# Split query and key operands for steps 3 and 4 of the first attention unit, and a later place for the second chunk's layer normalisation

## The chip, the cores and the metric

The kernel runs on one core of a Trainium2 chip. The metric is the time on the device in microseconds, median of several runs. TensorE (PE) multiplies matrices into PSUM, VectorE (DVE) and ScalarE (ACT) work on SBUF and PSUM, GpSimd (POOL) on SBUF alone, and SyncE (SP) issues the DMAs. Each engine takes its instructions in the order in which the program issued them, and waits at one whose inputs are not there yet.

## The reference

Layer normalisation, causal attention with 32 heads of 16, and a gate from a linear layer with routed low-rank corrections, on x of 2 x 1024 x 512 in float32:

```python
x = L0_attn_x                       # (2, 1024, 512)
xn = _layernorm(x, axis=-1)
q, k, v = (xn @ W.T + b for each)   # 32 heads of 16
scores = einsum('bhqd,bhkd->bhqk', q, k) / sqrt(16)
att = softmax(where(causal, scores, -inf))
s = (att @ v) @ Wo.T + bo
g = silu(xn @ W_base.T + b_base + top-2-of-8 routed rank-16 update)
return x + s * g
```

## The kernel before, in words

**Tiling.** The two sequences of 1024 tokens are cut into chunks of 512: (b, c). The heads are taken in four groups of 8 (oc). A *unit* (b, oc, c) is the attention of one group's heads for one chunk of queries. The first units are (0,0,0), (0,1,0), (0,0,1), (0,1,1). A unit is cut into *steps*; each step computes scores for some pieces of keys and queries (`scores`, L1714 on), takes their exponential on ScalarE in two instructions of 128 x 1024 (`pt`), masks the diagonal blocks on GpSimd (`masked`, L1756), and one step later multiplies by the values on TensorE (`values`, L1780). A unit of the first chunk has five steps: 0 and 1 take 512 columns for the even and the odd heads, 2 and 3 take pieces of 384 and 128 columns for the even and the odd heads, and 4 takes twice 256. So the plan's steps 0 to 4 are the first unit, and 5 to 9 the second. Score tiles have two PSUM buffers and a step uses both.

**Score operands.** All units but the first use *split* operands: queries and keys are cut into a rounded high part (`fp32r`) and a remainder, and a score is the sum of two reduced-precision matmuls. The heads of a pair share 32 rows, so the high parts and the remainders are interleaved: `split_keys` and `split_queries` write the high part on ScalarE and the remainder on VectorE, `copy_remainder` copies it on ScalarE, and `place_keys` and `place_queries` exchange rows by two DMAs each. The first unit, in `first_task`, uses whole float32 operands for all its five steps: `queries` writes two query tiles on VectorE, one for each parity of the heads with the other's rows zeroed, `keys` writes the keys on ScalarE. Its keys are split later (`apart`), since the third unit, the second chunk's queries for the same heads, reads them as split keys; `apart` shuffles the rows into pairs first, because `first_task` projects with weights in their plain order.

**Order.** The order of all instructions is written out by a planner when the program is built. The main loop issues, for each step n, the scores of n, the values of n-1, the masks of n, and then `fill(n)`: pieces of the other tasks (projections, values, gates, outputs). Inside `fill`, tasks with TensorE work come first, then the functions in the list `later` whose step has come, then those in `urgent`, and last the tasks without TensorE work. `turns` are called at its very start. A task gives way with `yield WAIT` (until the next fill) or `PAUSE`. `room` counts free buffers. The planner's own clock (`Metered`, `Queue`) decides only whether some of these functions are put off by a step; line L56 of the profile is the helper that issues nearly all VectorE and ScalarE instructions, L72 the one that issues SyncE's DMAs, L258 the helper of most matmuls.

**The stage at hand.** `early_values` (fills 0 to 2) makes the first chunk's values by a seven-product scheme on blocks: its products are p1, p2, p6, p7, p4, each followed by an addition on VectorE, and its last additions prepare the sums for p5 and p3 (`early_rest`, fills 3 and 4). In fill 2, behind `early_values`, `qk_task` projects queries and keys of the second unit (0,1,0) and splits them; its query remainder `qT<-qf,qT` on VectorE stands between two ScalarE operations. `layernorm_task(0, 1)` normalises the second chunk of the first sequence: statistics (fill 0), the power for the reciprocal deviation on GpSimd (L282), normalisation and the transposes of the first half in 32 x 32 blocks (fill 1), with a store of them to DRAM and four DMAs that bring them back with the blocks in place; the second half follows in fill 2. First read of the result: the projection of the third unit in fill 6.

Of the kernel before, what the change touches and what calls it, by code (L numbers as in the profile page):

```python
# [8 lines left out]
F32 = mybir.dt.float32  # L9
F32R = mybir.dt.float32r  # L10
# [21 lines left out]
NEG = -3.0e38  # L32
NF = 2 + 4 * 2 * 4
WARM = 10


Z_LOW, Z_HIGH = 1.0e-20, 1.0e20
# [60 lines left out]
def direct(ctx, tc, sound, x, wq, wk, wv, wo, wb, wa, wg, wB, bq, bk, bv, bo, bb, out):  # L98
# [148 lines left out]
    WAIT = object()  # L247
    PAUSE = object()
    turned_at, now = {}, [0]
    xns, xnTs, kTs, qTs, vs, gs, oTs, kfs = {}, {}, {}, {}, {}, {}, {}, []  # L250

    def mm_tile(name):
        return ps_mm.tile([P, D], F32, tag="mm", name=name)
# [42 lines left out]
    def layernorm_task(b, c):  # L296


        xt = chunk_tile(b, c)
        for i in range(NS):  # L300
            i0 = c * C + i * P
            sp.dma_start(
                out=xt[i * SQ : (i + 1) * SQ],
                in_=x[b, i0 : i0 + P].rearrange("(t r) d -> r t d", r=SQ),
            )
        if b == 0:
            load_rest()
        tiles = [xt[:, t] for t in range(TT)]
        for _ in range(3 if b else 1):
            yield WAIT  # L310
        s = yield from statistics(tiles, True)
        if b:
            yield WAIT
        for t in range(0, TT, 2):
            normalize(tiles[t : t + 2], s[0][:, t : t + 2], s[1][:, t : t + 2])
            yield PAUSE
        if b:
            yield WAIT
        xnT = sb.tile([P, KC, C], F32, tag="xnT", bufs=3, name=f"xnT_{b}_{c}")
        for k0 in range(0, KC, 2):  # L320
            sq = sb.tile([P, 2, NS, TT, SQ], F32, tag="sq", bufs=1, name="sq")
            for t in range(TT):
                yield PAUSE
                ve.transpose(
                    out=sq[:, :, :, t],
                    in_=tiles[t][:, k0 * P : (k0 + 2) * P].rearrange(
                        "p (k q d) -> p k q d", k=2, q=NS
                    ),
                )
            scr = dram.tile([NS, SQ, 2, NS, TT * SQ], F32, tag="scr", name="scr")  # L330

            def store(sq=sq, scr=scr, place=None):
                sp.dma_start(
                    out=scr.rearrange("i d k q m -> (i d) (k q m)"),
                    in_=sq.rearrange("p k q t r -> p (k q t r)"),
                )
                if place:
                    behind.append(place)
                    landed(place, now[0] + 3)

            def place(k0=k0, scr=scr):
                for q in range(NS):
# [9 lines left out]
            if not b:  # L352
                store()
                place()
                yield WAIT
                continue
            later.append((now[0] + b, lambda s=store, p=place: s(place=p)))
            for _ in range(0 if k0 else 1 + b):
                yield WAIT
        xnTs[b, c] = xnT  # L360

    def first_task():
# [4 lines left out]
        xnTs[0, 0], qTs[0, 0, 0] = xnT, qT  # L367
        kfs.append(kT)
# [60 lines left out]
        project_first(pq, wqks[0][:, 2 * KC : 3 * KC], TT - 1)  # L429
        queries(0)  # L430
        queries(1)
        ve.stream_shuffle(b_pair, b_sb, PAIRED)
        ve.tensor_tensor(b_less, b_pair[:, 0:KC], b_pair[:, KC:], ALU.subtract)
        project_first(pk, wqks[0][:, 3 * KC :], 3)
        keys(1, TT)
        kTs[0, 0, 0] = sb.tile([P, 2, C], F32R, tag="kT", bufs=4, name="kT_0_0_0")
        low = sb.tile([P, C], F32, tag="rb", bufs=1, name="low_0_0_0")

        def apart():
            ve.stream_shuffle(low, kT, PAIRED)  # L440
            split_keys(kTs[0, 0, 0], low, low)
            later.append((now[0] + 1, lambda: place_keys(kTs[0, 0, 0], low)))

        later.append((0, lambda: pair_up(wqks[1])))
        paired = lambda: pair_up(wqks[0])
        costs[paired], costs[apart] = (1.1, 5), (1.1, 6)
        later.append((3, paired))
        later.append((4, apart))
        yield 8 * MM

    def qk_task(b, oc, c):
# [401 lines left out]
    def early_values():  # L853

        at, raw, t, s = early_at["x"], early_at["w"], early_at["t"], early_at["s"]
        vt = value_tile(0, 0)
        for i in range(TT):
            vs[0, i] = vt[:, i]
        hv = heads(vt)
        early_at["v"] = slot = lambda i, j: hv[:, 2 * i : 2 * i + 2, H // 2 * j : H // 2 * (j + 1), 0:HD]  # L860
        s11, s12, s21, s22 = slot(0, 0), slot(0, 1), slot(1, 0), slot(1, 1)
        ve.tensor_tensor(s[1], at(1, 1), s[2], ALU.subtract)
        p1 = yield from early_product("p1", at(0, 0), raw[0, 0])
        early_add(s12, p1, early_bias(0))
# [12 lines left out]
        early_add(s21, p4, s21)  # L877
        ve.tensor_tensor(s[0], s[1], at(0, 0), ALU.add)
        ve.tensor_tensor(s[3], at(0, 1), s[1], ALU.subtract)
        ve.tensor_tensor(s12, s12, early_bias(1), ALU.add)  # L880

    def early_rest():

# [603 lines left out]
    for b in range(NB):  # L1487
        for c in range(NC):
            s0 = starts[b, 0, c]
            xn = [("xnT", b, c)]  # L1490
            if not b and not c:
                room["x"] -= 1
                Task(1, first_task(), 8 * MM, takes={"xnT": 1, "qT": 1, "kT": 1}, uses=xn)
            else:
                Task(
                    s0 - (12 if c else 25) if b else -9, layernorm_task(b, c), 0.0, after=s0 - (44 if c == 0 else 30) if b else -9,
# [217 lines left out]
    def scores(n):  # L1714
# [1 line left out]
        place_urgent(n)  # L1716
        ss = [ps_s.tile([P, 2, C], F32, tag="s", name=f"s{p}") for p in range(2)]
        for m, (par, kt, q0, w, col) in enumerate(pieces):
            first_unit = (b, oc, c) == units[0]
            halves = 1 if first_unit else 2  # L1720
            keys = kfs[0] if first_unit else kTs[b, oc, kt // TT][:, par]
            q = qTs[b, oc, c]
            for half_ in range(halves):
                for s in range(4):
                    rows = slice(32 * s, 32 * s + 32)
# [581 lines left out]
```

## Time and profile before

| | |
|---|---|
| median of 3 runs | 543.24 us (543.08 to 543.8) |
| profiled execution, its own time | 543.99 us |
| its span, first to last instruction | 542.2 us |
| granted TensorE clock | 0.995 |
| TensorE busy | 532.7 us (98%) |
| VectorE busy | 341.2 us (63%) |
| ScalarE busy | 351.4 us (65%) |
| GpSimd busy | 115.5 us (21%) |
| steps 3 and 4 of the first unit, start of scores | 37.35 and 41.16 us |
| first score of the second unit | 44.96 us |

Times are from the span's start. In a timeline a row gives start, duration, engine, line, operation, what is written and read, and in brackets the idle time of the engine before it and what ended it. Rows of one kind that follow one another are merged, with their count behind an x. Consecutive instructions of an engine overlap by some hundredths of a microsecond, so starts are better compared with starts. In the chain that ended last, durations are counted without overlap.

### The profile page before, as it was taken

Reading aid. Unit: us, or ns where it says so; the run is one execution under the profiler, and the core shown is the slowest. Engines: PE = TensorE matmul, PEld = TensorE weight load, DVE = VectorE, ACT = ScalarE, POOL = GpSimd, SP = SyncE. Lnnn points to the kernel's source line nnn. Section 1 sums busy time; section 2 is a strip of 40 time slices with the busy share of each in tenths; the row PEclk is TensorE's granted clock in tenths of the full one; section 3 lists DMA queues with packets and bytes.
Section 4 is the critical chain, followed back from the end, with each engine's and each line's share of the span. In section 5 each row is a group of like instructions: output and inputs, shape, how many; then the busy total and the mean of one; then the engine's idle time right before and its main releaser. Section 6 shows DMA issues by size and latency. Waiting matters only on the chain.

```text
span 542.2 us, 19903 instructions
## 1 busy us (share of the span) xinstructions
PE 532.7 (98%) x8623; PEld 284.1 (52%) x8623; DVE 341.2 (63%) x706; ACT 351.4 (65%) x387; POOL 115.5 (21%) x249
## 2 busy tenths in 40 slices
PE   8999999999999999999999999999999999999994
PEld 8546445544455554454555554454645564455672
DVE  5763586665584886566369766574276554749843
ACT  2457755777776766757667756657667776877640
POOL 2212401021033322030133320130113330121200
PEclk9999999999999999999999999999999999999997
DMA  8636366366526574813666545640124121753311
GB/s 252 158 110 211 133 165 223 91 197 205 160 99 215 195 226 155 230 42 100 187 169 199 186 135 171 195 149 24 63 97 143 61 85 28 253 169 91 101 41 48
DMA packets 67744, 78.15 MB, mean 144 GB/s; under 512 B 9928, under 2 KB 52944, under 8 KB 67136
## 3 DMA queue, kind: packets, MB, share of 16 engines
q1 hardware_dynamic: 67632, 76.78, 45.5%
q8 instruction: 70, 1.15, 0.9%
q14 instruction: 26, 0.21, 0.1%
q10 hardware_dynamic: 16, 0.00, 0.0%
HBM read 45.34 MB, written 19.37 MB: 119 GB/s over the span
## 4 chain that ended last, share of the span: by engine, by line
PE 97%; DVE 1%; DMA 1%; issue 0%; SPq 0%; POOL 0%; POOLq 0%
PE av L1780 26%; PE p L258 26%; PE s L1728 18%; PE q L258 14%; PE ph L258 3%; PE po L258 2%; PE pk L258 1%; PE pq L258 1%; PE warm L213 1%; PE pq_first L388 1%; PE h L258 1%; PE pk_first L388 1%; DMA kept<-w_gate 1%; PE pt_o L258 0%; PE pt_x L378 0%; DVE g L56 0%
## 5 line engine op out<-in xcount | busy, mean ns | idle before, releaser
L56 ACT ACTIVATE pt<-s 128x1024 f32<-128x1024 f32 x288 | 290.5, 1024 | 149.1 <-PE s L1728 145.6
L1756 POOL TENSOR_SCALAR_AFFINE_SELECT pt<-pt 128x256 f32<-128x256 f32 (+1 forms) x224 | 106.8, 491 | 400.0 <-ACT pt L56 399.5
L1780 PE MATMUL av<-pt,v 128*32 128x512 f32 (+3 forms) x1680 | 154.6, 467 | 0.1
L1728 PE MATMUL s<-qT,kT 32*128 32x512 f32 (+3 forms) x1616 | 106.6, 363 | 0.0
L1728 PEld LDWEIGHTS s<-qT,kT 32*128 32x128 f32 x1616 | 61.1, 183 | 56.6 <-issue 34.6
L1780 PEld LDWEIGHTS av<-pt,v 128*32 128x32 f32 x1680 | 40.8, 109 | 53.8 <-issue 38.5
L258 PE MATMUL p<-wt,asum 128*32 128x256 f32 x960 | 58.4, 379 | 0.0
L258 PE MATMUL q<-asum,wqk 128*32 128x256 f32 x832 | 51.1, 379 | 0.0
L258 PEld LDWEIGHTS p<-wt,asum 128*32 128x32 f32 x960 | 31.1, 110 | 29.2 <-issue 12.6
L258 PE MATMUL q<-xnT,wqk 128*32 128x256 f32 x624 | 39.5, 379 | 0.0
L258 PEld LDWEIGHTS q<-asum,wqk 128*32 128x32 f32 x832 | 26.8, 110 | 23.7 <-issue 6.6
L258 PEld LDWEIGHTS q<-xnT,wqk 128*32 128x32 f32 x624 | 20.2, 110 | 18.4 <-issue 6.6
L56 DVE SCALAR_TENSOR_TENSOR kf<-q,kf 128x256 f32<-128x256 f32 x39 | 16.5, 422 | 20.6 <-PE q L258 20.0
L56 DVE TENSOR_TENSOR g<-p,g 128x512 f32<-128x512 f32 x20 | 13.8, 688 | 22.8 <-PE p L258 22.6
L258 PE MATMUL p<-w,xnT 128*32 128x256 f32 x448 | 27.6, 379 | 0.0
L56 DVE TENSOR_TENSOR v<-p,v 128x512 f32<-128x512 f32 x22 | 15.0, 684 | 14.0 <-PE p L258 13.9
L258 PE MATMUL p<-w,asum 128*32 128x256 f32 x320 | 20.9, 379 | 0.0
L258 PEld LDWEIGHTS p<-w,xnT 128*32 128x32 f32 x448 | 14.9, 110 | 10.6 <-issue 3.3
L258 PEld LDWEIGHTS ph<-wag_sb,xnT 128*32 128x32 f32 x512 | 15.2, 110 | 3.9 <-issue 3.0
L56 DVE TENSOR_TENSOR x<-p,x 128x512 f32<-128x512 f32 x15 | 10.3, 685 | 10.4 <-PE p L258 10.4
L258 PE MATMUL ph<-wag_sb,xnT 128*32 128x136 f32 x512 | 16.6, 279 | 0.0
L56 DVE TENSOR_TENSOR g<-p,bb_sb 128x512 f32<-128x512 f32 x8 | 5.5, 690 | 17.2 <-PE p L258 17.1
(159 smaller groups left out, 577.5 us busy)
## 6 DMA issues: line engine op xcount, KB each, us to landing
wt<-kept SPq DMA_DIRECT2D x36, 256.0 KB
qT<-qT SPq DMA_DIRECT2D x30, 256.0 KB
x<-in_x_dram SPq DMA_DIRECT2D x16, 256.0 KB
kept<-wqk SPq DMA_DIRECT2D x16, 256.0 KB
wqk<-kept SPq DMA_DIRECT2D x4, 1024.0 KB
kT<-kf SPq DMA_DIRECT2D x30, 128.0 KB
scr<-sq SPq DMA_DIRECT2D x6, 512.0 KB
xnT<-scr SPq DMA_DIRECT2D x24, 128.0 KB
```

The source lines that it names most:

```text
L56: return getattr(self.engine, name)(*args, **named)
L213: nc.tensor.matmul(warm[:, n % 4 * P : n % 4 * P + P], lhsT=ident, rhs=ident, start=True, stop=True)
L258: nc.tensor.matmul(o[j : j + 32], lhsT=lhsT[:, j : j + 32] if len(lhsT.shape) == 2 else lhsT[:, j // 32], rhs=rhs, start=start, stop=stop,)
L388: nc.tensor.matmul(ps[:, cols], lhsT=w[:, k, :], rhs=xnT[:, k, cols], start=k == 0, stop=k == KC - 1)
L1728: nc.tensor.matmul(ss[s // 2][:, s % 2, col : col + w], lhsT=keys[rows, kt % TT * P : kt % TT * P + P], rhs=q[rows, halves * par + half_, ...
L1756: nc.gpsimd.affine_select(out=d, in_=d, compare_op=ALU.is_ge, fill=0.0, base=0, pattern=[[0, d.shape[1]], [1, P]], channel_multiplier=-1,)
L1780: nc.tensor.matmul(avs_now[par][32 * s : 32 * s + 32, q0 : q0 + w], lhsT=vs[b, kt][:, h * VS - HD * par : h * VS - HD * par + HP], rhs=pt[ ...
```

## The change

The first unit uses whole operands in steps 0 to 2 only (`SPLIT_FROM = 3`). For steps 3 and 4 its queries and keys are split like those of the other units. For that, ScalarE writes the queries with their bias from PSUM once more (`qf`), and `apart`, now in fill 0 instead of fill 6, shuffles both queries and keys into pairs on VectorE and splits both; the keys' placement, the queries' remainder and the queries' placement follow in fill 1. `first_task` takes both query buffers, and gives one back at the start of fill 2.

The second chunk's layer normalisation is moved for the first sequence. Its statistics are in fill 1 and no longer fill 0, with the power straight behind them. Normalisation and the first half's transposes and store (`begin`, `half(0)`) are called at the end of `early_values`, in fill 2, so that on VectorE they stand ahead of `qk_task`'s remainders. The placement of the first half is issued at the end of fill 2, and the second half's transposes, store and placement in fill 3.

```diff
+SPLIT_FROM = 3
...
     def layernorm_task(b, c):
-        for _ in range(3 if b else 1):
+        for _ in range(3 if b else 2):
             yield WAIT
-        s = yield from statistics(tiles, True)
-        if b:
+        s = yield from statistics(tiles, bool(b))
+        if b == 0:
+            xnT = sb.tile([P, KC, C], F32, tag="xnT", bufs=3, name=f"xnT_{b}_{c}")
+
+            def begin():
+                normalize(tiles, *s)
+                early_at["turn"] = half(0)
+
+            def half(k0):
+                sq = sb.tile([P, 2, NS, TT, SQ], F32, tag="sq", bufs=1, name="sq")
+                for t in range(TT):
+                    ve.transpose(
+                        out=sq[:, :, :, t],
+                        in_=tiles[t][:, k0 * P : (k0 + 2) * P].rearrange(
+                            "p (k q d) -> p k q d", k=2, q=NS
+                        ),
+                    )
+                scr = dram.tile([NS, SQ, 2, NS, TT * SQ], F32, tag="scr", name="scr")
+                sp.dma_start(
+                    out=scr.rearrange("i d k q m -> (i d) (k q m)"),
+                    in_=sq.rearrange("p k q t r -> p (k q t r)"),
+                )
+                return lambda: place_half(k0, scr)
+
+            def place_half(k0, scr):
+                for q in range(NS):
+                    sp.dma_start(
+                        out=xnT[q * SQ : (q + 1) * SQ, k0 : k0 + 2].rearrange(
+                            "d k (i m) -> d k i m", i=NS
+                        ),
+                        in_=scr[:, :, :, q].rearrange("i d k m -> d k i m"),
+                    )
+                if k0:
+                    turned_at[b, c] = now[0] + int((sp.landing() - sp.now) / 3.4)
+
+            early_at["begin"] = begin
+            while "turn" not in early_at:
+                yield WAIT
+            early_at["turn"]()
             yield WAIT
+            half(2)()
+            xnTs[b, c] = xnT
+            return
...
     def first_task():
         queries(0)
         queries(1)
+        qf = sb.tile([P, C], F32, tag="qf", bufs=2, name="qf_0_0_0")
+        act.activation(qf, pq, AF.Identity, bias=bq_sb[:, 0:1])
...
-        kTs[0, 0, 0] = sb.tile([P, 2, C], F32R, tag="kT", bufs=4, name="kT_0_0_0")
+        q2, k2 = split_tiles(0, 0, 0)
         low = sb.tile([P, C], F32, tag="rb", bufs=1, name="low_0_0_0")
+        turns.append((SPLIT_FROM - 1, lambda: room.update(qT=room["qT"] + 1)))
 
         def apart():
+            qs = sb.tile([P, C], F32, tag="qf", bufs=2, name="qs_0_0_0")
             ve.stream_shuffle(low, kT, PAIRED)
-            split_keys(kTs[0, 0, 0], low, low)
-            later.append((now[0] + 1, lambda: place_keys(kTs[0, 0, 0], low)))
+            ve.stream_shuffle(qs, qf, PAIRED)
+            split_keys(k2, low, low)
+            split_queries(q2, qs)
+            later.append((now[0] + 1, lambda: place_keys(k2, low)))
+            later.append((now[0] + 1, remainder))
+
+        def remainder():
+            copy_remainder(q2)
+            urgent.append((now[0], lambda: place_queries(q2)))
 
         later.append((0, lambda: pair_up(wqks[1])))
-        costs[paired], costs[apart] = (1.1, 5), (1.1, 6)
+        costs[paired] = 1.1, 5
+        later.append((0, apart))
         later.append((3, paired))
-        later.append((4, apart))
...
     def early_values():
         ve.tensor_tensor(s12, s12, early_bias(1), ALU.add)
+        early_at["begin"]()
...
-                Task(1, first_task(), 8 * MM, takes={"xnT": 1, "qT": 1, "kT": 1}, uses=xn)
+                Task(1, first_task(), 8 * MM, takes={"xnT": 1, "qT": 2, "kT": 1}, uses=xn)
...
     def scores(n):
-            first_unit = (b, oc, c) == units[0]
-            halves = 1 if first_unit else 2
-            keys = kfs[0] if first_unit else kTs[b, oc, kt // TT][:, par]
-            q = qTs[b, oc, c]
+            whole = n < SPLIT_FROM
+            halves = 1 if whole else 2
+            keys = whole_first[1] if whole else kTs[b, oc, kt // TT][:, par]
+            q = whole_first[0] if whole else qTs[b, oc, c]
```

More of the change, by code (lines that the diff above doesn't have):

```diff
@@ L249, in direct @@
     turned_at, now = {}, [0]
-    xns, xnTs, kTs, qTs, vs, gs, oTs, kfs = {}, {}, {}, {}, {}, {}, {}, []
+    xns, xnTs, kTs, qTs, vs, gs, oTs, whole_first = {}, {}, {}, {}, {}, {}, {}, []
     def mm_tile(name):
@@ L308, in layernorm_task @@
         tiles = [xt[:, t] for t in range(TT)]
[L309 removed]
+        for _ in range(3 if b else 2):
             yield WAIT
[L311 to L312 removed]
+        s = yield from statistics(tiles, bool(b))
[33 more added lines that the diff above has]
+            early_at["turn"]()
             yield WAIT
+            half(2)()
+            xnTs[b, c] = xnT
+            return
+        yield WAIT
         for t in range(0, TT, 2):
@@ L316, in layernorm_task @@
             yield PAUSE
-        if b:
-            yield WAIT
+        yield WAIT
         xnT = sb.tile([P, KC, C], F32, tag="xnT", bufs=3, name=f"xnT_{b}_{c}")
@@ L350, in place @@
                     turned_at[b, c] = now[0] + int((sp.landing() - sp.now) / 3.4)
[L352 to L356, printed above, removed]
             later.append((now[0] + b, lambda s=store, p=place: s(place=p)))
@@ L366, in first_task @@
         kT = sb.tile([P, C], F32, tag="kf", bufs=2, name="kf_0_0_0")
-        xnTs[0, 0], qTs[0, 0, 0] = xnT, qT
-        kfs.append(kT)
+        xnTs[0, 0] = xnT
+        whole_first.extend((qT, kT))
         pq = ps_av.tile([P, C], F32, tag="av", name="pq_first")
```

## The prediction

> **What bounds the kernel.** I read the page's busy shares, then the chain that ended last, then one timeline per engine from 15 to 62 us, where every edit falls.
>
> ```profile
> PE 532.7 (98%) x8623; PEld 284.1 (52%) x8623; DVE 341.2 (63%) x706; ACT 351.4 (65%) x387; POOL 115.5 (21%) x249
> ...
> PE 97%; DVE 1%; DMA 1%; issue 0%; SPq 0%; POOL 0%; POOLq 0%
> ```
>
> TensorE is busy for 98% of the span and is 97% of the chain. So a step counts in two ways only: TensorE work taken away, and TensorE made to wait. The other engines have room on average, but each TensorE step hangs on a ScalarE step: one step's scores can't be written before the step before has been exponentiated, since the score tiles have two buffers and a step takes both. The chain (start us, us) shows the stage:
>
> ```profile
> 37.42 1.08 PE s L1728 x16
> 38.50 1.00 PE av L1780 x16
> 39.50 1.73 PE p L258 x32
> 41.23 1.07 PE s L1728 x16
> 42.30 1.00 PE av L1780 x16
> ...
> 57.23 0.73 PE s L1728 x16
> ...
> 62.39 0.68 PE s L1728 x12
> ```
>
> Rows 1 and 4 are the scores of steps 3 and 4, the ones changed. 57.23 and 62.39 are the second unit's steps of the same shapes (384+128 columns, twice 256), with split operands already. Now the weight load ahead of row 4, and ScalarE before it (start us, us):
>
> ```profile
> 41.16 0.74 PEld L1728 LDWEIGHTS s<-qT,kf 32*128 32x128 f32 x16 [0.41 <-ACT pt L56]
> ```
>
> ```profile
> 34.78 1.06 ACT L56 ACTIVATE qT<-qf 128x1024 fp32r<-128x1024 f32 x1
> 36.59 0.63 ACT L56 ACTIVATE qT<-qT 128x512 fp32r<-128x512 f32 x1 [0.76 <-DVE qT L56]
> 37.49 0.69 ACT L56 ACTIVATE kf<-pk,b_pair 128x512 f32<-128x512 f32 x1 [0.27 <-PE pk L258]
> 38.21 1.06 ACT L56 ACTIVATE kT<-kf 128x1024 fp32r<-128x1024 f32 x1
> 39.17 1.92 ACT L56 ACTIVATE pt<-s 128x1024 f32<-128x1024 f32 x2
> ```
>
> Step 3's exponentials end at 39.17 + 1.92 = 41.09; step 4's weights load at 41.16, just as TensorE comes free (41.23). There is no slack: any delay of this ScalarE row lands on TensorE. Ahead of the exponentials in ScalarE's order stand five operations of the second unit's projection, and the second of them waits for VectorE:
>
> ```profile
> 22.24 0.69 DVE L56 BATCH_NORM_STATS2 st<-x 128x6 f32<-128x512 f32 x1
> ...
> 25.64 0.68 DVE L56 TENSOR_TENSOR v<-p,v 128x512 f32<-128x512 f32 x1
> ...
> 27.55 0.69 DVE L56 TENSOR_TENSOR v<-v,bv_sb 128x512 f32<-128x512 f32 x1
> 28.16 2.00 DVE L56 TENSOR_SCALAR x<-x,mv,rstd 128x512 f32<-128x512 f32 x4
> 30.08 1.41 DVE L56 STREAM_TRANSPOSE sq<-x 128x256 f32<-128x256 f32 x4
> 31.42 0.65 DVE L56 TENSOR_TENSOR v<-p,v 128x512 f32<-128x512 f32 x1
> ...
> 33.19 0.68 DVE L56 TENSOR_TENSOR v<-v,bv_sb 128x512 f32<-128x512 f32 x1
> 35.87 0.69 DVE L56 TENSOR_TENSOR qT<-qf,qT 128x512 fp32r<-128x512 f32 x1 [2.00 <-ACT qT L56]
> ```
>
> The last row is the second unit's query remainder. VectorE idles 2.00 us ahead of it. That hole is all the room there is.
>
> **Scores of steps 3 and 4 (gain).** 1.08 to 0.73 and 1.07 to 0.68: 0.35 + 0.39 = 0.74 us off TensorE. The Trainium skill ("FP8 and Floating Point Precision", TensorE Precision Notes) gives true FP32 four passes; two single-pass halves would then halve the time and give 0.54 twice, 1.08. The rows are of the same shapes, so I take 0.74.
>
> **The first unit's split, now right after step 0.** Before, its shuffle stands at 47.55 (0.75), its ScalarE copy at 52.30 (1.06), its subtraction at 53.40 (0.69). Now there are, at about 22.24: two shuffles, ending near 23.7; two ScalarE copies of 1.06 (keys from 23.05, queries to 25.1); two subtractions, ending near 25.8. The statistics that stood there took VectorE 22.24 to 25.64 and move away, so the next addition goes at about 25.7 instead of 25.64: under 0.1 us. Step 1's exponentials, queued behind on ScalarE, go from 22.77 to about 25.0 and end at 26.95. Step 2's scores load weights at 27.12 and step 1's masks end near 27.45 for values that start at 28.20: hidden by 0.17 and 0.75 us, and microsecond for microsecond beyond that. The ScalarE remainder (0.63) follows at about 27 in idle time, and four DMAs go out by 28.7 on a queue that stands empty from 18.5 to 31.5; the first reader is step 3 at 37.4. The new biased query copy (0.69) reads the projection's PSUM tile after VectorE: another such pair reads one after the other (VectorE's kf<-pk starts at 63.61, right as ScalarE's kT<-pk ends). So it runs at about 17.2 to 17.9 and pushes step 0's exponentials to an end near 20.3; their scores' buffers are wanted at 21.60. Hidden too. What is taken from 47 to 57 us was hidden already: nothing.
>
> **Statistics, normalisation, first transposes (loss).** Statistics move one step on, behind the addition at 27.55: from 28.16, for 25.64 − 22.24 = 3.40, to 31.56. The group of four additions that stood at 31.42 keeps its place (2.38 start to start, to 33.94). Then come normalisation and transposes, 31.42 − 28.16 = 3.26, to 37.20. Only now the query remainder, at 37.20 instead of 35.87: the hole holds 2.00 of 3.3 and it is 1.33 late. Behind it, in order: ScalarE's remainder copy 36.59 to 37.92; kf, which had waited for TensorE till 37.49, to about 38.5 (1.0 late, 0.3 is absorbed); kT; step 3's exponentials, ending 42.1 instead of 41.09. TensorE, faster by step 3's 0.35, comes to step 4 at 40.88. Two of its sixteen score matmuls can start on the first tile at 41.2; the others wait for 42.16 and end about 42.9, where before it was 42.30. So the wait is about 1.3, against 0.74 gained: **+0.6** net. Step 3's masks (1.68 before) end near 42.9 and hold its values by 0.05 at most.
>
> **GpSimd's queue.** The power for the reciprocal deviation moves from 25.82 to about 31.7, ahead of step 2's masks, which slip from 29.46 to 32.8. The values that read them come at 38.15, so that alone is free. But it now runs under VectorE's additions. Four masks under additions with two SBUF operands took 2.82 us instead of 1.75:
>
> ```profile
> 29.46 1.75 POOL L1756 TENSOR_SCALAR_AFFINE_SELECT pt<-pt 128x256 f32<-128x256 f32 x4 [2.62 <-ACT pt L56]
> ...
> 54.84 2.82 POOL L1756 TENSOR_SCALAR_AFFINE_SELECT pt<-pt 128x256 f32<-128x256 f32 x4 [2.80 <-ACT pt L56]
> ```
>
> The Trainium skill ("SBUF — State Buffer", SBUF: two separate sides) says why that speaks against the change: VectorE and GpSimd share one port pair as an exclusive lock, and the loser blocks for the whole instruction. By the rule in full, the power waits out the additions to 33.9, and normalisation starts 1.0 later. By the rows, both sides go on, VectorE's operations under masks at 0.77 and 0.88 instead of 0.69. I take 0.15 for the stretch, with 0 and 1.0 as ends.
>
> **SyncE's queue.** The first store moves from 31.52 to 37.3, query and key placements to about 38.6 and 41.0 (each 1.0 or less late; step 5's scores at about 45.7 need them), and the first half's placement now stands behind both, to 44.8. The second transposes move behind step 3, about 41.1; their store and placement (which follows 2.95 after its store at 41.35 and 44.30) go out by 50.8, the four kept stores by 53 instead of 49.1, the value weights by 57 instead of 53.1, the first unit's denominators near 62 instead of 57.69. First readers: the second chunk's projection at 51.88 (its second half near 56) and VectorE's sums at 54, the value weights at 63.9, VectorE's reciprocal at 67.46. Each is met by 2 us or more, and the queue has a hole from 58 to 61.4: nothing. The second chunk counts as turned in step 4 in both kernels (2 + 2 before; 3 + 1 by the same formula now), so TensorE's order stays.
>
> **Sum.** −0.74 + 1.3 + 0.05 + 0.15 is about +0.75. The profiled execution took 543.99 with a span of 542.2; this would make 544.7 and 542.95. Its 543.99 is 0.75 above the median, and the difference is carried over unscaled: 543.24 + 0.75 = **544.0**. Later stages have no TensorE idle time that could take it back.
>
> **Rivals.** *The remainder's delay is hidden*, and only the shorter scores count: 542.5. Speaks for it that VectorE and ScalarE are at 63 and 65%; against it that row 4 has no slack even now, so that the exponentials would have to end 0.2 earlier than today. Chance 0.10, most of it within 0.2%. *The port pair is held* (slower side): the power ends at 35 instead of 32.7, everything from normalisation on is 1.0 later, +1.75, 545.0; it decides from 0.35 us on. Chance 0.15. *SyncE's backlog reaches a reader*: the second chunk's second half, out at 50.8, lands after 56 and TensorE waits; some 1 to 2 us more, 545 to 546. The store-to-placement gaps of 3 to 4 us speak against it. Chance 0.08. *The order of steps changes* with the edited bookkeeping and the change is not what it looks like: either sign, around 1 us. Chance 0.05. The forecast keeps 0.62, with its own range 543.4 to 544.6.
>
> **Numbers.** 0.2% is 1.09 us, about what a measurement of this kernel can tell from no change: 542.15 to 544.33. Of the forecast's 0.62, 0.50 lie inside and 0.12 above. Same: 0.50 + 0.08. Slower: 0.12 + 0.15 + 0.08 + 0.02 = 0.37. Faster: 0.02 + 0.03. The range 542.7 to 545.2 leaves out the best case and the worst of the late ones.
>
> **What would show it.** Right: scores of steps 3 and 4 at 0.73 and 0.68 of work; VectorE's remainder near 37.2 with no idle time ahead of it; step 3's exponentials ending near 42.1; TensorE idle about 1.3 us within step 4's scores, and at most 0.1 anywhere else before 62 us. Wrong: no such idle time, the power ending after 33, or a new TensorE wait for a transfer past 50 us.

## The result, and the profile after

The changed kernel takes 544.46 us, median of 8 runs (544.25 to 546.42), against 542.86 for the kernel before on the same chip (8 runs, 542.62 to 543.8). The ratio is 1.0036, 95% interval 1.0025 to 1.0047: **slower by about 0.36%**, more than the 0.2% that can be told from no change. The forecast of 544.0 was half a microsecond low, and the likeliest case, "within 0.2%" (0.58), was not the one that came; "slower" had 0.37. As a change, +0.75 was forecast and +1.60 measured, more than twice as much. The time looks nearer than that because the kernel before came out at 542.86 here, 0.38 below the 543.24 that the forecast started from.

The eight executions fall in two groups: five at 544.25 to 544.55, three at 545.88 to 546.42. A second set of five, below, splits in the same way (three at 544.26 to 544.70, two at 545.98 and 546.09). Of the 31 executions of the kernel before that stand beside that second set none is above 543.51. What the longer group is comes further down.

Busy shares and the chain's shares by engine, of the kernel after:

```profile
PE 532.8 (98%) x8623; PEld 284.6 (52%) x8623; DVE 343.0 (63%) x709; ACT 353.1 (65%) x390; POOL 116.4 (21%) x249
...
PE 95%; DVE 3%; ACT 1%; issue 1%; POOL 0%; DVEq 0%; POOLq 0%; ACTq 0%
```

TensorE still has 8623 matmuls, but its share of the chain fell from 97 to 95%, and VectorE and ScalarE came into it. ScalarE has three instructions more (387 to 390), which will matter too; VectorE also has three more (706 to 709). Where they came into the chain (start us, us):

```profile
34.42 2.00 DVE x L57 x4
36.42 1.33 DVE sq L57 x4
37.76 0.58 DVE qT L57
...
38.36 0.63 ACT qT L57
38.99 0.58 ACT kf L57
...
40.56 1.93 ACT pt L57 x2
...
42.54 0.74 PE s L1776 x12
43.27 1.04 PE av L1828 x14
44.31 1.84 PE p L259 x30
46.15 0.67 PE s L1776 x6
```

From normalisation (`x`) over the first transposes (`sq`), the query remainder (`qT` on VectorE, then ScalarE) and step 3's exponentials (`pt`) it goes to step 4's scores, as foreseen. The last row, step 5's first scores, is at 46.15 instead of 45.03. Step 2's exponentials start at 28.31 after and at 28.36 before; this serves to align traces, and makes the stage's loss **1.16 us** (1.17 by the chain's rounded rows). TensorE's timeline of the kernel after has the loss in one place:

```profile
37.31 0.80 PE L1776 MATMUL s<-qT,kT 32*128 32x384 f32 x16
38.03 1.07 PE L1828 MATMUL av<-pt,v 128*32 128x384 f32 x16
38.92 1.91 PE L259 MATMUL p<-wt,asum 128*32 128x256 f32 x32
41.62 0.38 PE L1776 MATMUL s<-qT,kT 32*128 32x256 f32 x2 [0.79 <-ACT pt L57]
42.54 0.74 PE L1776 MATMUL s<-qT,kT 32*128 32x256 f32 x14 [0.53 <-ACT pt L57]
```

Step 3's scores now take 0.72 from start to start of the next row, where they took 1.08 (37.35 to 38.43 before). Step 4's scores would start at 40.76 (1.84 behind the projection, as before) and be done 0.68 later; values start at 43.20. So 43.20 − 40.76 − 0.68 = 1.76 us are lost. Only 0.79 + 0.53 = 1.32 of them stand as idle time. Between the two waits a pair of matmuls shows as 0.38 of work, but that pair saved next to nothing: the other fourteen took 0.66 (42.54 to 43.20), where all sixteen take 0.68. So its 0.38 is part of the loss.

VectorE's timeline of the kernel after, where the delay arises:

```profile
32.71 0.91 DVE L57 TENSOR_TENSOR asum<-xnT,asum 128x512 f32<-128x512 f32 x1
33.54 0.89 DVE L57 TENSOR_TENSOR v<-v,bv_sb 128x512 f32<-128x512 f32 x1
34.35 2.08 DVE L57 TENSOR_SCALAR x<-x,mv,rstd 128x512 f32<-128x512 f32 x4
...
37.68 0.65 DVE L57 TENSOR_TENSOR qT<-qf,qT 128x512 fp32r<-128x512 f32 x1
```

There is no idle time ahead of the remainder; the hole of 2.00 is used up. It goes at 37.68, not 37.20, and all of that 0.48 arises at the two additions of 0.91 and 0.89 (0.69 each otherwise) and in what follows straight behind. GpSimd in the same time, step 2's masks one by one:

```profile
31.68 1.02 POOL L283 TENSOR_TENSOR rstd<-rstd,mhalf 128x4 f32<-128x4 f32 x1 [4.42 <-DVE rstd L57]
32.66 0.41 POOL L1804 TENSOR_SCALAR_AFFINE_SELECT pt<-pt 128x256 f32<-128x256 f32 x1
33.02 0.85 POOL L1804 TENSOR_SCALAR_AFFINE_SELECT pt<-pt 128x256 f32<-128x256 f32 x1
33.84 0.85 POOL L1804 TENSOR_SCALAR_AFFINE_SELECT pt<-pt 128x256 f32<-128x256 f32 x1
34.65 0.58 POOL L1804 TENSOR_SCALAR_AFFINE_SELECT pt<-pt 128x256 f32<-128x256 f32 x1
...
41.64 1.68 POOL L1804 TENSOR_SCALAR_AFFINE_SELECT pt<-pt 128x256 f32<-128x256 f32 x4 [6.41 <-ACT pt L57]
```

The power ends at 32.70, as said. Step 2's four masks lie under the two additions and the start of normalisation, and take 2.57 together instead of 1.75. One by one, masks and additions take turns: mask, addition, mask, addition and mask end at 33.07, 33.62, 33.87, 34.43 and 34.69, so an addition always ends about 0.55 after the mask ahead of it, and a mask about 0.26 after the addition ahead of it. Step 3's masks, last row, end at 43.32; the values that read them begin at 43.20, and values and projection together take 46.15 − 43.27 = 2.88 in the chain instead of 2.73: another 0.15.

The stage closes: −0.36 and −0.39 for the scores, +1.76, +0.15, in all +1.16. Up to 526 us it stays so. Then the chain, around the last unit's values (after):

```profile
530.24 1.11 PE av L1828 x30
...
531.89 0.43 PE pt_o L259 x8
```

From 530.24 to 531.89 it is 1.65; the same piece took 1.37 before (529.11 to 530.48). ScalarE's timeline of the kernel after says why:

```profile
528.03 1.03 ACT L57 ACTIVATE pt<-s 128x1024 f32<-128x1024 f32 x1 [4.13 <-PE s L1776]
529.31 1.02 ACT L57 ACTIVATE pt<-s 128x1024 f32<-128x1024 f32 x1 [0.26 <-PE pt_o L259]
```

Between the last step's two exponentials ScalarE pauses for 0.26 us. Before, the two are one row, 526.90 to 528.93, with no gap. The last VectorE operation ends 1.40 us later than before (537.80 against 536.40): 1.16 of the stage, 0.28 here, less the shift of the start. The profiled spans differ by 0.5 alone because the profiled execution of before ended with a store that landed late; its 543.99 is 1.1 above its median beside the changed kernel.

### The profile page after: what moved, and what is told of

Same layout as the page of the kernel before. It is cut to its first block, busy times and chain, and to the rows that moved or that the text cites. A ratio compares the mean times of both kernels' runs of the same rounds, so it can differ in the third digit from the quotient of the medians.

```text
span 542.7 us, 19912 instructions
## 1 busy us (share of the span) xinstructions
PE 532.8 (98%) x8623; PEld 284.6 (52%) x8623; DVE 343.0 (63%) x709; ACT 353.1 (65%) x390; POOL 116.4 (21%) x249
## 4 chain that ended last, share of the span: by engine, by line
PE 95%; DVE 3%; ACT 1%; issue 1%; POOL 0%; DVEq 0%; POOLq 0%; ACTq 0%
PE av L1828 26%; PE p L259 25%; PE s L1776 18%; PE q L259 14%; PE ph L259 3%; PE po L259 3%; PE warm L214 1%; PE pq_first L424 1%; PE h L259 1%; PE pk_first L424 1%; PE pk L259 1%; PE pq L259 1%; PE pt_o L259 0%; PE pt_x L414 0%; DVE st L57 0%
## 5 line engine op out<-in xcount | busy, mean ns | idle before, releaser
L1776 PE MATMUL s<-qT,kT 32*128 32x512 f32 (+3 forms) x1648 | 108.5, 362 | 1.3 <-ACT pt L57 1.3
L1776 PEld LDWEIGHTS s<-qT,kT 32*128 32x128 f32 x1648 | 62.5, 183 | 59.4 <-issue 35.5
L57 DVE TENSOR_TENSOR g<-p,bb_sb 128x512 f32<-128x512 f32 x8 | 5.5, 690 | 17.2 <-PE p L259 17.1
```

The lines of the kernel that those rows point to most:

```text
L57: return getattr(self.engine, name)(*args, **named)
L1776: nc.tensor.matmul(ss[s // 2][:, s % 2, col : col + w], lhsT=keys[rows, kt % TT * P : kt % TT * P + P], rhs=q[rows, halves * par + half_, ...
```

## The experiments

In the expectations, A is the theory of the record: the remainder's place on VectorE makes the loss. B puts it on the first unit's split, squeezed in after step 0, C on SyncE's later transfers, P on ScalarE's pauses, G on the TensorE clock after a wait. Each ratio is against the kernel before on the same chip; a shift of the stage is that of step 5's scores, aligned by step 2's exponentials (by its scores where the exponentials themselves have moved).

| run | median us | before | ratio (95%) | stage |
|---|---|---|---|---|
| changed kernel again | 544.70 | 543.05 | 1.0042 (1.0028 to 1.0056) | +1.16 |
| layer normalisation moved, no split | 544.62 | 543.05 | 1.0032 (1.0020 to 1.0044) | +1.42 |
| normalisation behind the remainder | 543.02 | 543.05 | 1.0003 (0.9995 to 1.0012) | −0.27 |
| power behind the masks | 543.85 | 543.05 | 1.0016 (1.0009 to 1.0023) | +0.58 |
| split, layer normalisation as before | 548.11 | 543.05 | 1.0095 (1.0079 to 1.0110) | |
| behind the remainder, keys rounded from PSUM | 542.72 | 543.05 | 0.9995 (0.9986 to 1.0004) | −0.36 |
| before, three small ScalarE copies more | 543.34 | 543.05 | 1.0006 (0.9997 to 1.0015) | 0.0 |
| changed kernel, keys written twice | 547.45 | 543.05 | 1.0077 (1.0063 to 1.0091) | +3.95 |
| split spread over VectorE's gaps | 542.30 | 543.12 | 0.9986 (0.9979 to 0.9992) | −0.75 |
| before, keys rounded from PSUM | 543.28 | 543.12 | 1.0002 (0.9994 to 1.0010) | |

**The changed kernel again**, for the spread of its executions.

> The changed kernel once more, on the same chip as the three edits of it. Theory A (the second unit's query remainder is late on VectorE, so step 3's exponentials are late and TensorE waits in step 4): step 5's scores begin near 46.15 in the chain where they were at 45.03, and the time is 1.1 to 1.6 us above the kernel before. Theory B (the first unit's split, squeezed in after step 0, makes TensorE wait by itself): the same numbers. Theory C (the first transfers of the second chunk come too late): the same start of step 5, but TensorE idle behind 50 us, and a time that differs from chip to chip.

The loss is there again, and so are the two groups. The mean granted clock of an execution goes with them: 0.994 or 0.995 in the five of 545.88 to 546.42, 0.996 to 0.998 in the other eight of the two sets. The group means are 546.13 and 544.39, and the mean clocks 0.9944 and 0.9975; 0.0031 of 543 us is 1.7 us, the difference of 1.74. A single mean says little, though: the profiled execution of the kernel before has 0.995 as well, because the clock is at half behind 537 us, where TensorE has no work left. Both profiled executions of the changed kernel fell in the shorter group, so the fall itself has to be looked for in a kernel that has it always; the run with a longer wait, below, does that.

**One part alone: the layer normalisation moved, without the split.**

```diff
 (the kernel before, with the changed kernel's layernorm_task)
     def early_values():
...
+        early_at["begin"]()
```

> The kernel before with the second chunk's layer normalisation moved as in the change, and the first unit whole in all five steps. A: the remainder still goes at 37.2 to 37.7, step 3's exponentials end near 42.4, step 4's whole scores end near 43.5 (before 42.30), step 5 begins near 46.2; time +1.2 us against the kernel before. B: nothing of the split is there, so 0. C: above 0 only if TensorE waits behind 50 us.

The move alone costs the stage 1.42, and the time +0.32%; B, which foresaw no loss here, falls. The split's shorter scores, 0.74 of work, give back 0.26. TensorE's timeline:

```profile
41.16 0.70 PE L1764 MATMUL s<-qT,kf 32*128 32x256 f32 x4 [0.45 <-ACT pt L56]
42.07 1.13 PE L1764 MATMUL s<-qT,kf 32*128 32x256 f32 x12 [0.21 <-ACT pt L56]
```

What TensorE saves by the shorter scores it mostly spends waiting for the same exponentials: step 3's end 14.18 after the start of step 2's here, and 14.17 in the changed kernel. The pause at the end is not in this trace (387 ScalarE instructions, as before).

**Undo the order alone: normalisation behind the remainder.** All of the change, but `begin` is called once the second unit's query remainder has been issued.

```diff
     def early_values():
-        early_at["begin"]()
...
     def qk_task(b, oc, c):
         split_queries(qT, qf)
+        if (b, oc, c) == units[1]:
+            early_at["begin"]()
```

> The changed kernel with normalisation, first transposes and their store behind the second unit's query remainder instead of in front of it; nothing else. A: the remainder goes at 35.9, step 3's exponentials end near 41.1, TensorE waits about 0.3 in step 4, step 5 begins near 44.6, and the time is 0.4 us below the kernel before. B: the split is unchanged, so the time stays 1 us or more above. C: the transposes come 2 us later still, so it gets worse than the change, +2 or more.

```profile
35.39 0.69 DVE L57 TENSOR_TENSOR qT<-qf,qT 128x512 fp32r<-128x512 f32 x1 [1.38 <-ACT qT L57]
...
38.70 1.92 ACT L57 ACTIVATE pt<-s 128x1024 f32<-128x1024 f32 x2
...
40.67 0.53 PEld L1777 LDWEIGHTS s<-qT,kT 32*128 32x128 f32 x14 [0.15 <-ACT pt L57]
```

(VectorE, ScalarE and weight loads.) The remainder has idle time ahead of it again, exponentials end at 40.62, and the wait in step 4 is 0.15. The time is back at that of before, although the first store after normalisation goes out 1.9 us later still than in the changed kernel, so C falls; A stands. But −0.4 was expected, and it is a miss: the stage gained 0.27 only, since TensorE still reaches step 4 ahead of the exponentials, and two pauses of ScalarE, at step 48 (0.2) and at the last step (0.28), took it back.

**The masks and the additions.** The power is issued in `begin`, behind step 2's masks, so that these run ahead of the two additions.

```diff
     def statistics(xs, apart=False, between=None, power=True):
...
+        if power:
+            raise_power(rstd, nt)
...
             def begin():
+                raise_power(s[1], TT)
                 normalize(tiles, *s)
```

> The changed kernel with GpSimd's power for the second chunk issued in front of the normalisation, so behind step 2's masks, and no longer between the statistics and those masks. A with the shared port: step 2's masks run before VectorE's two-operand additions again, those take 0.68 instead of 0.9, the remainder goes near 37.3 instead of 37.68, step 5 begins near 45.75, and the time is 0.4 us below the change. Rival (the additions are long for another reason, or the power itself holds the port): no gain over the change.

GpSimd's timeline, then VectorE's:

```profile
28.90 0.77 POOL L1809 TENSOR_SCALAR_AFFINE_SELECT pt<-pt 128x256 f32<-128x256 f32 x2 [2.14 <-ACT pt L57]
...
31.19 1.02 POOL L288 TENSOR_TENSOR rstd<-rstd,mhalf 128x4 f32<-128x4 f32 x1 [0.52 <-DVE rstd L57]
```

```profile
32.21 0.69 DVE L57 TENSOR_TENSOR asum<-xnT,asum 128x512 f32<-128x512 f32 x1
32.82 0.69 DVE L57 TENSOR_TENSOR v<-v,bv_sb 128x512 f32<-128x512 f32 x1
...
36.59 0.65 DVE L57 TENSOR_TENSOR qT<-qf,qT 128x512 fp32r<-128x512 f32 x1
```

Masks and additions no longer meet: 0.77 for two masks, 0.69 for both additions. Step 2's exponentials start at 27.81 here, 0.50 ahead of the changed kernel's trace, so the remainder goes at 37.09 on the changed kernel's scale, 0.59 sooner, and the stage's loss falls from 1.16 to 0.58. So the meeting of masks and additions costs 0.59, and the power itself, which still lies beside VectorE's work, is not what did it. TensorE's waits in step 4 are 0.20 and 0.53 here, and none of the 18 executions falls in a longer group (the highest is 544.9, at a mean clock of 0.997).

**The other part alone: the split, with the layer normalisation as before.** The statistics then stand behind the split on VectorE.

> The split of the change with the second chunk's layer normalisation left where it was before (statistics in fill 0, now behind the split's shuffles and subtractions on VectorE). A: the statistics end 3.4 us later and the addition after them goes at about 29 instead of 25.64; TensorE's next product, which wants that PSUM tile, waits about 3.3 us near 26.5; step 4 then waits 0.3 at most; time +2.5 to +3 us against the kernel before. Rival (VectorE has room enough, and the move of the normalisation was the only harm): TensorE doesn't wait, and the time is 0.4 to 0.7 us below the kernel before.

TensorE's timeline, then a table of stretches (stretch, length, busy of PE, PEld, DVE, ACT and POOL, granted clock, DMA share, GB/s):

```profile
29.39 1.03 PE L259 MATMUL p<-wt,xnT 128*32 128x256 f32 x8 [3.04 <-DVE v L57]
30.35 2.09 PE L1740 MATMUL s<-qT,kf 32*128 32x384 f32 x16
```

```profile
26.10:29.51 3.41, 0.37 (x12) 0.12 (x8) 3.17 (x10) 0.85 (x2) 1.09 (x2) 1.00 0.49 192
29.51:32.92 3.41, 3.41 (x28) 1.46 (x30) 3.38 (x7) 0.39 (x1) 0.34 (x1) 0.50 0.01 2
```

Where the split stands, there is no room for 3.4 us of statistics: the addition behind them, on which TensorE waits for its PSUM buffer, is late by 3. So the statistics had to move if the split goes there; what did not have to move is normalisation ahead of the remainder. The time is +5.1, not +2.5 to 3: right after the wait the granted clock is 0.50, for 3.41 us. From the first of these rows to the end of the values behind the second, 29.39 to 33.51, TensorE takes 4.12 us for what took 2.51 before (26.57 to 29.08): 1.61 for the clock.

**A longer wait.** To see whether the clock also explains the changed kernel's longer executions, its wait is made longer by one more ScalarE instruction of 1.06 us: the second unit's high keys are written twice.

```diff
     def qk_task(b, oc, c):
...
             act.activation(kf, pk, AF.Identity, bias=bias_k)
+            act.activation(kT, kf.unsqueeze(1).to_broadcast([P, 2, C]), AF.Copy)
             split_keys(kT, kf, kf)
```

> The changed kernel with the second unit's rounded keys written twice by ScalarE (1.06 us more, the same values), so that step 3's exponentials and TensorE's wait in step 4 grow by about 0.96. Some executions of the changed kernel took 1.7 us more than the others, at a mean granted clock of 0.994 instead of 0.998, and none of the kernel before did. A alone: +0.96 against the change, 2.4 us above the kernel before. Theory G (TensorE's wait of about 1.3 us in step 4 is now and then long enough for the clock to be halved for a few us): with a longer wait most or all executions are at about 0.994, the profile shows a granted clock below 1 just behind step 4, and the time is about 4.1 us above the kernel before.

```profile
42.63 0.38 PE L1777 MATMUL s<-qT,kT 32*128 32x256 f32 x2 [1.90 <-ACT pt L57]
43.54 0.74 PE L1777 MATMUL s<-qT,kT 32*128 32x256 f32 x14 [0.53 <-ACT pt L57]
...
45.74 3.10 PE L259 MATMUL p<-wv,asum 128*32 128x256 f32 x29
```

```profile
41.36:44.77 3.41, 1.61 (x24) 1.18 (x28) 3.08 (x7) 2.62 (x4) 1.54 (x4) 1.00 0.21 77
44.77:48.18 3.41, 3.41 (x40) 2.54 (x36) 0.12 (x1) 1.56 (x2) 1.27 (x2) 0.50 0.62 180
48.18:51.59 3.41, 3.41 (x78) 2.22 (x73) 2.14 (x4) 1.97 (x3) 0.41 (x1) 1.00 0.34 132
```

(TensorE, then stretches with the columns of above.) The idle time grew by 1.11, and then the clock fell to 0.50 at 44.77 and came back at 48.18, 3.41 us later: the projection's 29 matmuls took 3.10, 1.89 in the changed kernel. In the chain, values and projection took 4.56 instead of 2.88: 1.68 for the clock. Half of 3.41 is 1.71, so this is an estimate of what one such fall costs while TensorE has work throughout; 1.61 in the run above and the 1.74 between the changed kernel's two groups lie near it. With the 1.16 of the changed kernel that makes 3.95 for the stage, which is what step 5's scores show. G's 4.1 was right for the time (+4.2 to +4.4), A's 2.4 was not.

**Three ScalarE instructions more, in the kernel before.**

```diff
+        pad = small.tile([P, 1], F32, tag="pad", bufs=1, name="pad")
+        for _ in range(3):
+            act.copy(pad, mhalf)
```

> The kernel before with three ScalarE copies of 128x1 more, in ScalarE's idle time at 12 us; nothing else. The four kernels with the split have three ScalarE instructions more than the kernel before and all show a pause of 0.26 us between step 143's two exponentials, which the kernel before hasn't. Theory P (ScalarE pauses at fixed counts of its instructions, and three more of them move a pause onto step 143, which nothing hides): the pause of 0.26 is there too, and the time is 0.2 to 0.3 us above the kernel before. Rival (it is a consequence of the later stage): no pause, same time.

```profile
526.52 1.03 ACT L56 ACTIVATE pt<-s 128x1024 f32<-128x1024 f32 x1 [4.13 <-PE s L1731]
527.81 1.03 ACT L56 ACTIVATE pt<-s 128x1024 f32<-128x1024 f32 x1 [0.26 <-PE pt_o L258]
```

The pause is at the last step now, in the kernel before, with nothing else changed, and the stage at step 4 is where it was. In the chain the same piece takes 1.64 (528.74 to 530.38) instead of 1.37. The time rose by 0.3, as P says, though the interval of the ratio holds no change too. So the pause goes with the number of ScalarE instructions. Between a step's two exponentials, every trace with 390 of them has one at steps 61, 114 and 143, the last of them in the open; the two with 387 have one at step 88, where it is hidden; those with 386 and 391 have one at step 34 and one at 33, and the two with 389 have none there. Why ScalarE pauses there was not tried.

**Room on ScalarE besides.** As the kernel with normalisation behind the remainder, and the second unit's high keys are rounded straight from PSUM in one ScalarE operation (the other units of the second chunk do so already).

```diff
-        if c:
+        if c or (b, oc, c) == units[1]:
```

> As the run with the normalisation behind the query remainder, and the second unit's keys are rounded by ScalarE straight from PSUM, with the unrounded copy made by VectorE, as the third unit does: one ScalarE operation of 0.69 fewer ahead of step 3's exponentials. A: those end near 40.4, step 4's scores don't wait at all, step 5 begins 0.74 us earlier than before (near 44.3 on the clock of the kernel before), and the time is 0.5 to 0.7 us below the kernel before. B or C (the split or the transfers make TensorE wait elsewhere): no better than the kernel before.

A miss: 0.9995 is not clear of no change. Step 4's scores wait for nothing here. Of the 0.74 that the scores save, the stage keeps 0.36, since other waits come up behind it: a mask that takes 0.84 beside VectorE's key subtraction costs 0.25, and the landing of the keys 0.07. Then the third unit comes to the second chunk's second half before it has landed, as an addition on VectorE that waits for the same transfer shows:

```profile
54.62 0.69 DVE L57 TENSOR_TENSOR asum<-xnT,asum 128x512 f32<-128x512 f32 x1 [5.81 <-DMA xnT<-scr]
```

The third unit's projection reads that transfer too: in the chain its second half starts at 54.63, and the 24 matmuls take 2.99 against 2.76 in the kernel before. So SyncE's later transfers, harmless in the changed kernel, are a bound as soon as the stage ahead is mended: what the rival of the record said, one step on.

**The split spread over VectorE's gaps.** Layer normalisation stays as it was. The shuffles come at the end of `first_task`, where VectorE is idle; the high parts on ScalarE in fill 0; and the two subtractions one step later, ahead of normalisation. The keys are rounded from PSUM.

```diff
+        qs = sb.tile([P, C], F32, tag="qf", bufs=2, name="qs_0_0_0")
+        ve.stream_shuffle(qs, qf, PAIRED)
+        ve.stream_shuffle(low, kT, PAIRED)
...
         def apart():
+            act.activation(k2, low.unsqueeze(1).to_broadcast([P, 2, C]), AF.Copy)
+            high = q2.rearrange("p (a h) c -> p a h c", a=2)[:, :, 0]
+            act.activation(high, qs.unsqueeze(1).to_broadcast([P, 2, C]), AF.Copy)
+            later.append((now[0] + 1, subtract))
+
+        def subtract():
+            ve.tensor_tensor(low, low, k2[:, 0].bitcast(F32), ALU.subtract)
+            ve.tensor_tensor(q2[:, 1], qs, q2[:, 0].bitcast(F32), ALU.subtract)
+            place_keys(k2, low)
+            remainder()
```

> The split of steps 3 and 4, with the second chunk's layer normalisation where it was in the kernel before, and the split's own VectorE work in the idle times there: both shuffles behind the first projection (near 18 us, before the first addition at 19.5), both subtractions one step later, in front of the normalisation (near 28.2 us), so that they take up part of the 2.00 us hole ahead of the second unit's query remainder. The second unit's keys are rounded straight from PSUM. A: the remainder stays at 35.9, nothing waits in step 4, SyncE's first store is 1.3 us late and not 6, step 5 begins 0.74 us earlier than before, and the time is 0.6 to 0.8 us below the kernel before. Rival (the split can't be had without a wait somewhere): within 0.2 us of the kernel before or above.

The chain:

```profile
36.92 0.73 PE s L1747 x13
37.65 1.00 PE av L1799 x16
38.65 1.73 PE p L259 x32
40.38 0.67 PE s L1747 x16
...
43.78 0.67 PE s L1747 x8
```

TensorE alone, with no wait: 0.73 and 0.67 for the scores, 1.00 and 1.73 for what follows. Its step 2 starts 0.50 sooner in the trace than that of before, so the stage is at −0.75, just the 0.74 of work saved. The time is 542.30 against 543.12, **0.9986 (0.9979 to 0.9992)**: 0.8 us faster than before, the fastest of all. **The kernel before with only the keys rounded from PSUM** settles whose gain that is:

> The kernel before with the second unit's keys rounded straight from PSUM, whole operands in all five steps of the first unit. A: step 3's exponentials end 0.7 us earlier, but TensorE comes to step 4 no sooner, so the time is that of the kernel before, within 0.2 us; the gain of the run beside it is then the split's. Rival: the fused keys alone bring what that run gains.

1.0002 (0.9994 to 1.0010), no change: the keys alone bring nothing, and the gain comes with the split. Whether the split spread like this would keep all of it without the keys was not run; with 390 ScalarE instructions instead of 389 a pause at the last step would have to be reckoned with.

## Why the prediction was right, and where its sizes were not

**What bounds.** Right: the loss came through the row that was shown to have no slack, step 3's exponentials ahead of step 4's scores, and undoing the order alone took it away.

**Scores, −0.74.** Right by the rows: −0.36 and −0.39. Had they been halved (the four passes that were weighed against the rows), it would have been 1.08.

**The split, nothing.** Right in the changed kernel: step 1's exponentials from 24.87 (25.0 said), the query copy at 17.21 (17.2), and no TensorE wait there. But that nothing rested on the statistics leaving the spot, which only the run of the split alone shows: +5.1 us without it.

**The remainder, +1.3.** The mechanism is right, and the size by a coincidence of two readings. The sum meant the whole delay of TensorE, from 40.88 to 42.9 less 0.68. By that reading it was 1.76. The idle time in the brackets is 1.32, but it leaves out the 0.38 of the two matmuls between the waits. The missing 0.42 is nearly all lateness of the exponentials: they ended at 42.48 instead of 42.1.

**The port, +0.15.** This is the term that was mis-sized: "I take 0.15 for the stretch, with 0 and 1.0 as ends". The run with the power behind the masks puts the meeting of step 2's masks with VectorE's work at 0.59. The remainder was late against the forecast by 0.48 of that; about 0.1 was already in the rows that the forecast was worked out from, where masks ran beside normalisation. The row shown with the prediction, four masks in 2.82 instead of 1.75, was the same meeting. It was read as "both sides go on", and mostly for GpSimd's side, which has time. One by one those masks took 0.84, 0.85 and 0.85 beside additions and 0.40 alone, and they and the additions ended in turn, as in the kernel after. That agrees with the lock of the Trainium skill ("SBUF — State Buffer", SBUF: two separate sides), by which the one that starts first has the shared ports for its whole instruction and the other waits. But a turn is one mask and not the whole row: the two additions follow each other at 0.83 and 0.81 instead of 0.60, so each meeting cost VectorE about 0.2, and VectorE had no hole left to take that up. The prediction had tried the lock on the power instead. That ended on time, and beside it an addition with two SBUF operands (32.11 to 32.79) was not stretched either, so for the power the rows do not show the lock.

**Masks, +0.05.** It was 0.15, for the same reason: step 3's exponentials were later than said, so its masks ended at 43.32 and not at 42.9.

**SyncE's queue, nothing.** Right, with less to spare than said: the second half of the chunk had landed by 55.03, when an addition that waits for it starts, and TensorE reads it from 56.45 on: 1.4 us and not 2. In the version in which TensorE comes to it 1.5 sooner than in the changed kernel it is too late.

**"Later stages have no TensorE idle time that could take it back"** was right, but two things that add were not in the sum. ScalarE's three more instructions move its pauses, and one falls on the last step: +0.28. And in five of thirteen executions the clock falls after the wait: 5/13 of 1.74 is +0.67 in the mean.

**The account.** 1.16 + 0.28 = 1.44. The shorter groups of the two sets lie 1.38 and 1.40 above the mean of the kernel before beside them, so stage and pause account for them. With 0.67 for the clock it is 2.1 for all executions, against 1.95 and 2.28 by the two ratios. The forecast's +0.75 lacks 0.41 in the stage (port and masks), 0.28 at the end, and the clock. So the account was right in its path and its direction, and the measured time lies within the range of 542.7 to 545.2; its size was less than half. The clock's part in the changed kernel itself is inferred: the mean granted clocks of the two groups and the two longer waits speak for it, but no trace of the changed kernel in its longer group was taken.

**The rivals.** "The delay is hidden" (542.5) did not come, but the spread split, at 542.30, is that case made true. "The port pair is held" had the right place and put it on the wrong instruction, with a size of 1.0 instead of 0.6. No order of steps changed.

## What to carry to other kernels

When a group of instructions is moved ahead of one that another engine waits for, measure the idle time ahead of that one and subtract: 3.3 us into a hole of 2.0 is a loss, whatever the engine's busy share says. Where no hole is left, every lengthening by a neighbour counts in full, so look up what the group will then run beside. The same work cut into pieces that fit the holes, here two shuffles, two copies and two subtractions at three places, gave all of the gain that the scores had to give.

## What the runs showed of the hardware that was not expected

**The TensorE clock falls after short waits.** With idle times of 0.79 and 0.53, 0.38 of work between them, five of thirteen executions have the lower mean clock and 1.74 us more. With 1.90 and 0.53, and with 3.04 in one piece, the profiled execution shows the clock at 0.50 for 3.41 us after the wait, and it cost 1.6 to 1.7 us; all nine executions of these two kernels have a mean clock of 0.995 or less. With 0.20 and 0.53 (the power behind the masks) no execution of 18 was longer. The fall comes late: with the longer wait, at 44.77, 1.2 us after TensorE went on. What decides whether an execution of the changed kernel has it was not found. The Trainium skill ("TensorE: Matmul & The Clock Gate", Part 1: The HAM clock gate) has the clock at half after at least one idle window of about 3.4 us; here the waits were shorter. By that rule the longer wait would have cost 1.1 more than the changed kernel's; it cost 2.8.

**ScalarE pauses for about 0.26 us at places that go with the count of its instructions.** Three copies of 128 x 1 moved one from where it was hidden to where it cost 0.27 in the chain. What it waits for in the pause is open; the Trainium skill ("Runtime: NRT & Kernel Launch", Instruction fetch mechanics) calls the crossing into a new block of instructions mostly hidden, and whether this is such a crossing no run here shows.

**VectorE's additions and GpSimd's masks take turns, instruction by instruction.** Masks of 0.41 alone take 0.85 beside an addition, and each of the two additions that met them held up the next VectorE instruction by about 0.2.

**Idle time can understate a wait.** Two of the sixteen score matmuls ran before the second half of their input was there and show as 0.38 of work, but the other fourteen then took 0.66, where all sixteen take 0.68. The wait cost 1.76, and 1.32 of it stands as idle time.
